# Norm statistics on ScalarE and attention sums over pairs of steps: a graph-attention kernel bound by TensorE

## The chip, the cores and the metric

One core of a Trainium2 chip. The metric is the device time of one execution in microseconds (us). Times are medians of several executions; all of this study's executions are of the fast state, with granted TensorE clocks of 0.985 to 0.996. A ratio is the mean time of one kernel's runs over that of the other's of the same rounds, so it is not quite the ratio of the two medians. Its interval is a 95% interval.

In lines of the profile PE is TensorE, PEld its weight loads, DVE VectorE, ACT ScalarE, POOL GpSimd and SPq the queue that issues transfers (DMA); L1108 is line 1108 of that run's kernel. A timeline line gives the start in us, the length in us, engine, line, operation, what it writes and reads, shapes and count; square brackets give the idle time of the engine before it and what ended it.

## The reference

Sixteen graphs of 1024 nodes with 256 channels pass four layers, each `x = x + layer(relu(layernorm(x)))`. Three are graph attention (4, 1 and 1 heads), the fourth is masked attention with 8 heads and a feed-forward part that ends in a norm of its own.

```python
h = relu(_layernorm(x)); x = x + _L0_gnn_ref(h, adj, W, a)       # 4 heads
h = relu(_layernorm(x)); x = x + _L1_gnn_ref(h, adj, W, a)       # 1 head
h = relu(_layernorm(x)); x = x + _L2_gnn_ref(h, adj, W, a)       # 1 head
h = relu(_layernorm(x))
# _L3_gnn_ref(h): 8 heads of 32 channels
scores = where(adj > 0, q @ k.T / sqrt(D), -1e9)
t = softmax(scores) @ v
y = _layernorm(h + t) * g1 + c1
x = x + _layernorm(y + relu(y @ w1 + b1) @ w2 + b2) * g2 + c2
```

## The kernel before

The kernel first records every operation of all batches, with an estimated duration and a priority, and then lists them greedily: each engine takes, of what is ready, the operation with the smallest priority. The lists are fixed when the program is built. On the chip each engine works through its own list in order. The priorities come from a few knots (values between which it interpolates) per stage, shifted by a lead per engine:

```python
LANDING = 2.5                       # assumed us from a DMA's end of transfer to its use
BIAS = 0.648                        # weight of TensorE's cost of changing its array shape
LEAD = {"act": -0.527, "dve": 0.112}

def priority(x):
    base, knots, total, lead = x.stream          # base is the batch number
    ...
    return round(key - (LEAD.get(x.engine, 0.0) if lead else 0.0), 6)
```

Statistics of every norm were taken on VectorE:

```python
def stats(src, src_ref, dst, dst_ref, whose="g"):
    st = r_st[whose].new()
    dve(0.342, lambda: nc.vector.bn_stats(st.t, src), [st], [src_ref])
    dve(0.11, lambda: nc.vector.bn_aggr(dst, st.t), [dst_ref], [st])
```

The attention of the fourth layer runs in four groups per batch (two sets of four heads, two halves of the queries), each of eight steps over the keys. In a step TensorE makes four score matmuls, ScalarE takes their exps, VectorE multiplies by the mask, and TensorE multiplies by the values ("va") in a "quad": four matmuls side by side, each in 32 columns of the array. The sum of the weights for the softmax comes from a quad with ones. In a "paired" group VectorE first adds two steps, so that one quad of ones serves both:

```python
def paired(g, hf):
    return g == 1 or hf == 1        # the first group is not paired
...
both = not paired(g, hf)
pe((1 + both) * 0.855, lambda: value(m, both), ...)      # quad of va, and of ones if not paired
if not both and jt % 2:
    pe(0.855, lambda: quad(accs[g, hf][1], jt, ..., lambda r: ones, ...), ...)
...
if paired(g, hf) and jt % 2:
    for ss, p0, p1 in zip(sums[n], pas[n - 1], pas[n]):
        dve(tt_us(2 * HALF), lambda: nc.vector.tensor_add(ss.t, p0.t, p1.t), [ss], [p0, p1])
```

The last stage reads the rows of x back, adds the last norm's constant row, and later stores from the same buffer (a ring of two, `r_xr`):

```python
dma(1.15, lambda: nc.sync.dma_start(xr.t, x3.t[:, it : it + 2, :]), [xr(0), xr(1)], [x3(hf)])
dve(tt_us(2 * C), lambda: nc.vector.tensor_add(xr.t, xr.t, rows["c2"].to_broadcast([P, 2, C])), ...)
...
dma(0.65, lambda: nc.sync.dma_start(out[b]...[:, it : it + 2, :], xr.t), [], [xr(0), xr(1)])
```

## Time and profile before

| | before |
|---|---|
| time, median of 3 | 4209.74 us (4208.88 to 4213.89) |
| TensorE, VectorE, ScalarE busy | 98%, 88%, 55% |
| one batch in the steady part | 255.5 us |
| end of the last batch's layer-3 products to the end of the span | 197 us |

Busy shares are averages over a start, a steady part in which two batches interleave, and an end in which the last batch is alone. The lines that carry the reading stand in the prediction.

### The profile page before, as it was taken

What the parts mean: (1) busy time and instruction counts of PE and PEld (TensorE: products, weight loads), DVE (VectorE), ACT (ScalarE), POOL (GpSimd) and SP (SyncE); (2) the same over time, 40 slices, a digit from 0 to 9 for tenths busy, and PEclk for the clock granted to TensorE, in tenths of its full rate; (3) what the DMA queues carried; (4) which work ended last, traced back from release to release, by engine and by line L of the source; (5) the groups of instructions that cost most, each with busy time, mean ns of one, the idle gap of its engine ahead of it and who ended that gap; (6) DMA issues with size and microseconds to landing.
All of it is one profiled execution on the core that took longest, in us unless ns stands there. A gap on an engine that the chain in (4) does not pass through costs nothing.

```text
span 4208.8 us, 68595 instructions
## 1 busy us (share of the span) xinstructions
PE 4133.7 (98%) x24738; PEld 2399.0 (57%) x24738; DVE 3710.0 (88%) x6786; ACT 2333.7 (55%) x5041; POOL 427.2 (10%) x391
## 2 busy tenths in 40 slices
PE   7999999999999999999999999999999999999998
PEld 3746556564665646556465564646656465564643
DVE  7589898998989889898998979989898898989977
ACT  3445555564655746556555555646556465565564
POOL 0001001011010101001010010110111010010110
PEclk9999999999999999999999999999999999999998
DMA  3121222212222122221212222122221222212131
GB/s 104 48 64 42 81 61 66 66 36 81 58 74 61 51 65 57 76 71 52 66 45 81 61 66 66 36 81 59 73 60 50 65 58 76 69 49 67 44 86 36
DMA packets 180683, 263.82 MB, mean 63 GB/s; under 512 B 41328, under 2 KB 76400, under 8 KB 180336
## 3 DMA queue, kind: packets, MB, share of 16 engines
q1 hardware_dynamic: 180336, 259.36, 22.5%
q8 instruction: 198, 3.24, 0.3%
q14 instruction: 149, 1.22, 0.1%
HBM read 91.03 MB, written 33.95 MB: 30 GB/s over the span
## 4 chain that ended last, share of the span: by engine, by line
PE 80%; DVE 12%; DMA 2%; SPq 2%; issue 2%; POOL 1%; ACT 1%; DVEq 0%; ACTq 0%
PE bank L801 21%; PE bank L1108 16%; PE sc L1235 10%; PE bank L677 8%; DVE pt L774 7%; PE bank L875 6%; PE bank L474 5%; PE sc L1024 5%; PE bank L1341 4%; PE bank L885 3%; DVE pa L1268 2%; PE sc L1060 2%; SPq L1045 2%; DMA row<-rd 1%; POOL rstdz L426 1%
## 5 line engine op out<-in xcount | busy, mean ns | idle before, releaser
L1259 ACT ACTIVATE pa<-sc 128x512 f32<-128x512 f32 x2048 | 1096.4, 607 | 588.4 <-PE sc L1235 448.6
L1268 DVE TENSOR_TENSOR pa<-pa,mask 128x1024 f32<-128x1024 f32 x1024 | 1210.1, 1211 | 12.4 <-ACT pa L1259 12.0
L774 DVE SCALAR_TENSOR_TENSOR pt<-row,e,mask 128x512 f32<-128x512 f32 x1536 | 1058.5, 740 | 107.5 <-DMA row<-rd 78.6
L801 PE MATMUL bank<-qb,pt 128*128 128x257 f32 x4096 | 942.8, 381 | 0.5 <-ACT ex L829 0.4
L801 PEld LDWEIGHTS bank<-qb,pt 128*128 128x128 f32 x4096 | 770.6, 190 | 166.5 <-issue 21.8
L1235 PE MATMUL sc<-qs,ks 128*128 128x512 f32 x2048 | 700.4, 448 | 1.9 <-ACT pa L1259 1.3
L1108 PE MATMUL bank<-pa,va 128*32 128x512 f32 x4096 | 543.5, 597 | 7.4 <-DVE pa L1268 7.0
L875 PE MATMUL bank<-pt,qb 128*32 128x512 f32 x4096 | 511.5, 596 | 4.7 <-DVE pt L774 4.7
L1235 PEld LDWEIGHTS sc<-qs,ks 128*128 128x128 f32 x2048 | 358.0, 188 | 223.7 <-ACT pa L1259 102.7
L1283 DVE TENSOR_TENSOR sums<-pa,pa 128x1024 f32<-128x1024 f32 x384 | 454.6, 1213 | 7.0 <-PE bank L1108 6.5
L677 PE MATMUL bank<-w_aug,hT 128*128 128x259 f32 (+1 forms) x1536 | 372.8, 391 | 0.6 <-ACT mask L587 0.2
L426 POOL TENSOR_TENSOR rstd<-rstd,neg_half 128x4 f32<-128x4 f32 x160 | 200.7, 1257 | 1499.8 <-DVE rstd L423 1340.9
L677 PEld LDWEIGHTS bank<-w_aug,hT 128*128 128x128 f32 x1536 | 289.4, 192 | 94.4 <-issue 15.3
L875 PEld LDWEIGHTS bank<-pt,qb 128*32 128x32 f32 x4096 | 132.8, 109 | 303.4 <-issue 210.3
L829 ACT ACTIVATE ex<-bank,rec 128x256 f32<-128x256 f32 x256 | 121.6, 476 | 324.0 <-DVE rec L821 321.1
L885 PE MATMUL bank<-pt,e 128*32 128x512 f32 x2048 | 288.4, 593 | 0.0
L1108 PEld LDWEIGHTS bank<-pa,va 128*32 128x32 f32 x4096 | 118.8, 109 | 283.1 <-issue 196.5
L445 ACT ACTIVATE hn<-xt,mv,rstd 128x256 f32<-128x256 f32 x384 | 204.2, 598 | 87.7 <-DVE mv L435 87.7
L906 ACT COPY ot<-bank 128x512 f32<-128x512 f32 x128 | 75.0, 586 | 318.7 <-PE bank L875 269.7
L1024 PE MATMUL sc<-hTa,wqkv_sb 128*128 128x512 f32 x512 | 239.9, 595 | 1.0 <-ACT hTa L1009 0.5
L1108 PE MATMUL bank<-sums,ones 128*32 128x512 f32 x1536 | 216.4, 597 | 0.7
L417 DVE BATCH_NORM_STATS2 stg<-xt 128x6 f32<-128x256 f32 x512 | 208.9, 414 | 3.2
(107 smaller groups left out, 4053.0 us busy)
## 6 DMA issues: line engine op xcount, KB each, us to landing
row<-rd SPq DMA_DIRECT2D x192, 256.0 KB
ks<-hi SPq DMA_DIRECT2D x512, 64.0 KB
ks<-lo SPq DMA_DIRECT2D x512, 64.0 KB
qs<-hi SPq DMA_DIRECT2D x512, 64.0 KB
qs<-lo SPq DMA_DIRECT2D x512, 64.0 KB
xt<-in_x_dram SPq DMA_DIRECT2D x32, 512.0 KB
x<-xt SPq DMA_DIRECT2D x32, 512.0 KB
xr<-x SPq DMA_DIRECT2D x64, 256.0 KB
```

Source lines behind the costliest of these rows:

```text
L426: lambda: nc.gpsimd.tensor_tensor(out=rstd, in0=rstd, in1=neg_half[:, :n], op=ALU.pow),
L677: nc.tensor.matmul(g.t[:, : C + 3 * H], hT.t[:, ct, k * P : (k + 1) * P], w_aug[l][:, ct, :], start=ct == 0, stop=ct == CT - 1,)
L774: lambda: nc.vector.scalar_tensor_tensor(pt.t, row.t, e3[:, 2, jt // TH, h, jt % TH : jt % TH + 1], mask[:, jt, hf * HALF : (hf + 1) * HAL ...
L801: nc.tensor.matmul(g.t[:, : D + 1], pts[jt].t[:, k * P : (k + 1) * P], qb[:, jt, 0, :], start=jt == 0, stop=jt == NT - 1,)
L875: nc.tensor.matmul(g.t[u * D + d : u * D + d + D3, :], qb[:, j, h + u, d : d + D3], pts[u][j - jt].t, start=j == 0, stop=j == NT - 1,)
L885: nc.tensor.matmul(gd.t[c : c + D3, :], one(jt + k, h + u).to_broadcast([P, D3]), pts[u][k].t, start=jt == 0, stop=jt == NT - 2,)
L1024: nc.tensor.matmul(sc.t, wqkv_sb[:, ct, c0 : c0 + P], hT.t[:, ct, hf * HALF : (hf + 1) * HALF], start=ct == 0, stop=ct == CT - 1,)
L1108: nc.tensor.matmul(ac.t[r * D3 : (r + 1) * D3, :], columns(r), of_head(r), start=first, stop=last,)
L1235: nc.tensor.matmul(scs[r - r0].t, ks.t[:, r, jt * P : (jt + 1) * P].bitcast(F32R), q.t[:, r, :].bitcast(F32R), start=True, stop=True,)
L1259: lambda: nc.scalar.activation(pt.t[:, v, :], sc.t, AF.Exp, scale=1.0 / math.sqrt(D3)),
L1268: lambda: nc.vector.tensor_mul(pt.t, pt.t, mask[:, jt : jt + 1, i0 : i0 + HALF].to_broadcast([P, 2, HALF]),),
L1283: lambda: nc.vector.tensor_add(ss.t, p0.t, p1.t),
```

## The change

The intent: take statistics off VectorE, which is 88% busy, give them to ScalarE, which is 55% busy, and spend what VectorE gains on pairing all sums, which takes quads of ones off TensorE. In the last batch, where VectorE is the fuller engine, nothing is paired. All priorities are set anew.

```diff
-BIAS = 0.648
-LEAD = {"act": -0.527, "dve": 0.112}
+BIAS = 0.977
+LEAD = {"act": 2.43, "dve": 0.791}
 ...  (all knots of GATS, VALUES, STEPS and FEED are new)
+    waste = ring("waste", 1, [C]).new()
+    SQUARED = (0, 2, 3,)
+    def spread_of(srcs, src_refs, sums, squares, refs):
+        act(0.19, lambda: nc.scalar.mul(sums, sums, -1.0 / C), refs, [])
+        for k, (src, src_ref, ref) in enumerate(zip(srcs, src_refs, refs)):
+            act(act_us(C, 1) + 60e-3,
+                lambda: nc.scalar.activation(waste.t, src, AF.Square,
+                    bias=sums[:, k : k + 1], accum_out=squares[:, k : k + 1]), [ref], [src_ref])
 ...  (one-head layers: the last residual operation gives the sum as well)
-                    stats(xs, xt(it), mv[:, l + 1, it, :], b_mv((l + 1, it)))
+                    dve(stt_us(C) + 60e-3,
+                        lambda: nc.vector.scalar_tensor_tensor(
+                            xs, xs, 0.0, last, op0=ALU.add, op1=op, accum_out=total), ...)
 ...
-            return g == 1 or hf == 1
+            return b < NB - 1
 ...  (last norm: two copies out of PSUM with a sum each, instead of one copy)
-                act(act_us(HALF), lambda: nc.scalar.copy(z_t, pz()), [z(0), z(1)], [g])
-                    stats(z_t[:, k, :], z(k), mvz.t[:, k, :], mvz(k), "f")
+                        lambda: nc.scalar.activation(
+                            z_t[:, k, :], pz()[:, k, :], AF.Copy, accum_out=mvz.t[:, k, 0:1])
 ...  (input norm)
-        for it in range(NT):
-            stats(xt.at(it), xt(it), b_mv.t[:, 0, it, :], b_mv((0, it)))
+            for it in its:
+                act(act_us(C) + 60e-3, lambda: nc.scalar.activation(
+                        waste.t, xt.at(it), AF.Copy, accum_out=b_mv.t[:, 0, it, 0:1]), ...)
+            spread_of(...)
```

The norms of the second layer's input and of the attention's sum keep bn_stats.

More of the change, by code (lines that the diff above doesn't have):

```diff
@@ L313, in direct @@
     GATS = (
-        (-0.447, -0.367, -0.162, 0.113, 0.24),
-        (0.384, 0.522, 0.626, 0.731, 0.828),
-        (0.805, 0.841, 0.856, 0.879, 1.02),
-    )
-    VALUES = (1.045, 1.057, 1.088, 1.245, 1.191)
-    STEPS = (1.289, 1.484, 1.664, 1.807, 1.951)
-    FEED = (2.178, 2.28, 2.353, 2.529, 2.38)
+        (-3.014, -2.567, -1.878, -0.484, 0.173),
+        (0.132, 0.454, 0.649, 0.709, 0.772),
+        (0.836, 0.897, 0.92, 0.922, 1.169),
+    )
+    VALUES = (1.226, 1.309, 1.09, 1.477, 0.846)
+    STEPS = (1.141, 1.486, 1.711, 1.952, 1.974)
+    FEED = (2.264, 2.344, 2.373, 2.44, 2.31)
     const = ctx.enter_context(tc.tile_pool(name="const", bufs=1))
@@ L418, in stats, with inverse_of_squares @@
         dve(0.11, lambda: nc.vector.bn_aggr(dst, st.t), [dst_ref], [st])
+    SQUARED = (0, 2, 3,)
+    def spread_of(srcs, src_refs, sums, squares, refs):
+        act(0.19, lambda: nc.scalar.mul(sums, sums, -1.0 / C), refs, [])
+        for k, (src, src_ref, ref) in enumerate(zip(srcs, src_refs, refs)):
+            act(
+                act_us(C, 1) + 60e-3,
+                lambda: nc.scalar.activation(
+                    waste.t, src, AF.Square, bias=sums[:, k : k + 1], accum_out=squares[:, k : k + 1]
+                ),
+                [ref],
+                [src_ref],
+            )
+    def inverse_of_squares(mean, squares, rstd, refs, rstd_ref, negate=True):
+        n = squares.shape[-1]
+        dve(
+            ts_us(n),
+            lambda: nc.vector.tensor_scalar(
+                rstd, squares, 1.0 / C, EPS, op0=ALU.mult, op1=ALU.add
+            ),
+            [rstd_ref],
+            refs,
+        )
+        pool(
+            0.98,
+            lambda: nc.gpsimd.tensor_tensor(
+                out=rstd, in0=rstd, in1=neg_half[:, :n], op=ALU.pow
+            ),
+            [rstd_ref],
+            [],
+        )
+        if negate:
+            dve(tt_us(n), lambda: nc.vector.tensor_mul(mean, mean, rstd), refs, [rstd_ref])
     def inverse(mean, var, rstd, mv_refs, rstd_ref, negate=True):
@@ L645, in gat @@
             mv_refs, rstd_ref = [b_mv((l, it)) for it in its], b_rstd((l, hf))
-            inverse(mv[:, l, s, 0], mv[:, l, s, 1], rstd[:, l, s], mv_refs, rstd_ref)
+            inv = inverse_of_squares if l in SQUARED else inverse
+            inv(mv[:, l, s, 0], mv[:, l, s, 1], rstd[:, l, s], mv_refs, rstd_ref)
             hn, hT = r_hn.new(), r_hT.new()
@@ L849, in gat @@
                     xs = xt.at(it)
-                    dve(tt_us(C), lambda: nc.vector.tensor_add(xs, xs, ex), [xt(it)], [b_ex(0)])
-                    if l != 1:
-                        dve(
-                            tt_us(C),
-                            lambda: nc.vector.tensor_sub(xs, xs, eo),
-                            [xt(it)],
-                            [b_ex(1)],
-                        )
-                    stats(xs, xt(it), mv[:, l + 1, it, :], b_mv((l + 1, it)))
+                    total = mv[:, l + 1, it, 0:1]
+                    if l == 1:
+                        last, op = ex, ALU.add
+                    else:
+                        dve(tt_us(C), lambda: nc.vector.tensor_add(xs, xs, ex), [xt(it)], [b_ex(0)])
+                        last, op = eo, ALU.subtract
+                    dve(
+                        stt_us(C) + 60e-3,
+                        lambda: nc.vector.scalar_tensor_tensor(
+                            xs, xs, 0.0, last, op0=ALU.add, op1=op, accum_out=total
+                        ),
+                        [xt(it), b_mv((l + 1, it))],
+                        [b_ex(int(l != 1))],
+                    )
+                its = range(hf * TH, (hf + 1) * TH)
+                spread_of(
+                    [xt.at(it) for it in its],
+                    [xt(it) for it in its],
+                    mv[:, l + 1, s, 0],
+                    mv[:, l + 1, s, 1],
+                    [b_mv((l + 1, it)) for it in its],
+                )
                 continue
@@ L982, in attention @@
             mv_refs, rstd_ref = [b_mv((3, it)) for it in its], b_rstd((3, hf))
-            inverse(mv[:, 3, s, 0], mv[:, 3, s, 1], rstd[:, 3, s], mv_refs, rstd_ref)
+            inv = inverse_of_squares if 3 in SQUARED else inverse
+            inv(mv[:, 3, s, 0], mv[:, 3, s, 1], rstd[:, 3, s], mv_refs, rstd_ref)
             for it in its:
@@ L1420, in back @@
                 pe(0.109 * 2 * CT, turn_back, [g], [yT])
-                act(act_us(HALF), lambda: nc.scalar.copy(z_t, pz()), [z(0), z(1)], [g])
                 for k in range(2):
-                    stats(z_t[:, k, :], z(k), mvz.t[:, k, :], mvz(k), "f")
-                inverse(
-                    mvz.t[:, :, 0], mvz.t[:, :, 1], rstdz.t, [mvz(0), mvz(1)], rstdz, False
+                    act(
+                        act_us(C) + 60e-3,
+                        lambda: nc.scalar.activation(
+                            z_t[:, k, :], pz()[:, k, :], AF.Copy, accum_out=mvz.t[:, k, 0:1]
+                        ),
+                        [z(k), mvz(k)],
+                        [g],
+                    )
+                refs = [mvz(0), mvz(1)]
+                spread_of(
+                    [z_t[:, k, :] for k in range(2)],
+                    [z(k) for k in range(2)],
+                    mvz.t[:, :, 0],
+                    mvz.t[:, :, 1],
+                    refs,
                 )
+                inverse_of_squares(mvz.t[:, :, 0], mvz.t[:, :, 1], rstdz.t, refs, rstdz, False)
                 for k in range(2):
@@ L1435, in back @@
                             rows["g2"][:, 0, :],
-                            op0=ALU.subtract,
+                            op0=ALU.add,
                             op1=ALU.mult,
@@ L1478, in batch @@
             )
-        for it in range(NT):
-            stats(xt.at(it), xt(it), b_mv.t[:, 0, it, :], b_mv((0, it)))
+        for hf in range(2):
+            its = range(hf * TH, (hf + 1) * TH)
+            for it in its:
+                act(
+                    act_us(C) + 60e-3,
+                    lambda: nc.scalar.activation(
+                        waste.t, xt.at(it), AF.Copy, accum_out=b_mv.t[:, 0, it, 0:1]
+                    ),
+                    [b_mv((0, it))],
+                    [xt(it)],
+                )
+            s = slice(hf * TH, (hf + 1) * TH)
+            spread_of(
+                [xt.at(it) for it in its],
+                [xt(it) for it in its],
+                b_mv.t[:, 0, s, 0],
+                b_mv.t[:, 0, s, 1],
+                [b_mv((0, it)) for it in its],
+            )
         for l in range(3):
```

## The prediction

> **What bounds the kernel now.** I read the page's engine shares first, then the groups by line and shape, then TensorE's own timeline, then the windows of the start and the end.
>
> ```profile
> span 4208.8 us, 68595 instructions
> PE 4133.7 (98%) x24738; PEld 2399.0 (57%) x24738; DVE 3710.0 (88%) x6786; ACT 2333.7 (55%) x5041; POOL 427.2 (10%) x391
> ```
>
> TensorE looks full, but the busy share of matmuls can mislead, so I measured it from distances between starts. In the timeline of TensorE (start, length, line, count):
>
> ```profile
> 1003.84 1.04 PE L885 MATMUL bank<-pt,e 128*32 128x512 f32 x8
> 1004.69 1.12 PE L1108 MATMUL bank<-pa,va 128*32 128x512 f32 x8
> 1005.55 1.12 PE L1108 MATMUL bank<-pa,ones 128*32 128x512 f32 x8
> 1006.60 1.09 PE L474 MATMUL bank<-ident,ot 128*128 128x128 f32 x8
> ```
>
> A "quad" (four matmuls side by side in 32-column strips, eight records because each fp32 matmul is two) takes 0.86 us from start to start, though the row says 1.12. I took the whole timeline from 400 to 3700 us and fitted, by least squares over the start-to-start distances, one duration for each kind of matmul and one for each kind of change between array shapes (full array, 32-column strips, the score matmuls). Result: 3189 us of matmuls, 70 us of changes of shape, 29 us of anything else, in 3289 us. So 97% of the steady part is matmul time and about 2.3 us per batch of some 255.6 us is waiting. (In the chain of work that ended last, the 12.18 us piece of L801 starts at 654.85 and, 13 batches later, at 3977.35: 255.6 us per batch.) The steady part is bound by TensorE's work. VectorE has 229 of 255 us filled in one batch, ScalarE 145.
>
> ```profile
> 455.00:710.00 255.00, 253.71 (x1544) 148.60 (x1543) 229.69 (x420) 144.89 (x314) 27.74 (x24) 1.00 0.23 63
> 4080.00:4120.00 40.00, 38.86 (x172) 13.74 (x168) 39.76 (x41) 24.07 (x46) 0.00 (x0) 1.00 0.39 97
> 4120.00:4160.00 40.00, 38.51 (x199) 13.14 (x198) 40.00 (x38) 24.84 (x48) 0.00 (x0) 1.00 0.06 14
> ```
>
> These windows give PE, PEld, DVE, ACT and POOL in turn. At the end, where the last batch is alone, the bound is another: from 4080 to 4160 VectorE has 79.8 of 80 us filled, and TensorE's pieces, counted with the fitted durations, are only about 54 us plus some 10 of changes.
>
> **What the Trainium skill says.**
> 1. "Perfetto Trace Analysis", opening note: matmul busy time is a bad measure, because matmuls are pipelined. Agreed here: 1.12 us recorded against 0.86 from start to start.
> 2. "TensorEngine Tiling (Array Packing)", Key Properties: changing the tiling mode drains TensorE. Agreed: in the fit a trip from the scores to the strips and back costs about 0.41 us, from the full array to the strips and back 0.22, and from the full array to the scores and back about nothing.
> 3. "ScalarE: Activation LUTs", What ACT_TABLE_LOAD costs: an ACTIVATE takes 186 ns plus 0.833 ns per element, plus 93 ns for each per-partition operand, and neighbours overlap by about 93 ns. For 256 elements that is 399 and 492 ns; the trace has 425 (no such operand, L843) and 476 (one, L829). It does not price the accumulator output. The built programs have one table load each, so Square brings no table switching.
> 4. "VectorE: DVE Perf Modes", Two Vector instructions with no wait between them: an op that writes out its accumulator is two instructions. No run shows it yet; I put 60 ns on it, as the kernel's own estimate does.
>
> **The change part by part.**
>
> ```profile
> L1268 DVE TENSOR_TENSOR pa<-pa,mask 128x1024 f32<-128x1024 f32 x1024 | 1210.1, 1211 | 12.4 <-ACT pa L1259 12.0
> L1283 DVE TENSOR_TENSOR sums<-pa,pa 128x1024 f32<-128x1024 f32 x384 | 454.6, 1213 | 7.0 <-PE bank L1108 6.5
> L1108 PE MATMUL bank<-sums,ones 128*32 128x512 f32 x1536 | 216.4, 597 | 0.7
> L1108 PE MATMUL bank<-pa,ones 128*32 128x512 f32 x1024 | 149.5, 593 | 0.0
> L417 DVE BATCH_NORM_STATS2 stg<-xt 128x6 f32<-128x256 f32 x512 | 208.9, 414 | 3.2
> L418 DVE BATCH_NORM_AGGREGATE mv<-stg 128x2 f32<-128x6 f32 x512 | 84.6, 168 | 2.3
> L850 DVE TENSOR_TENSOR xt<-xt,ex 128x256 f32<-128x256 f32 x256 | 105.8, 413 | 19.0 <-ACT ex L829 19.0
> ```
>
> (a) Attention sums. Each batch has four groups of eight steps. Before, the first group sums with one quad per step, the other three add pairs of steps on VectorE and take four quads. After, in 15 batches the first group is paired too: 4 quads less, 4 x 0.862 = 3.45 us per batch, 51.7 us in all, all on the bound engine. VectorE gets 8 adds more per batch, 8 x 1.213 = 9.7 us. The last batch loses its 24 adds (29 us of VectorE) and gets 12 quads (10.3 us).
>
> (b) Statistics. Gone from VectorE are 512 bn_stats (input, two layers, last norm) and as many aggregates: 384 x 0.414 + 128 x 0.408 + 512 x 0.167 = 297 us. The residual adds of two layers become scalar_tensor_tensor with an accumulator: 256 of them, about 0.468 (L1431, same size) + 0.06 against 0.413, so + 29 us. With the 96 more adds of (a), 116 us, VectorE's sum is -297 + 29 + 116 = -152, from 3710 to about 3560. In a steady batch: 229 + 9.7 - 18.5 + 1.8 = 222 us.
>
> (c) ScalarE gets 128 copies with a sum (about 0.485), 512 squares (0.536), 160 tiny scalings (0.19), and 64 copies of 512 are split in two: 62 + 274 + 30 + 22 = about 390 us of recorded time. From 145 to some 167 us of a batch. Off the path on average.
>
> (d) Order. All priorities are retuned. I compared the two built instruction streams: in batches 2 to 15 TensorE changes its array shape more often, 1353 times against 1177 over the 11 batches I counted alike. Weighted with the fitted costs, this is 71.7 against 59.9 us, 1.07 us per batch, 16 us over 15 batches. In the last batch's tail there are 72 changes against 84.
>
> (e) The tail. Where the last batch's first group runs unpaired, a step takes 3.0 us:
>
> ```profile
> 4055.13 1.33 PE L1235 MATMUL sc<-qs,ks 128*128 128x512 f32 x4
> 4056.39 1.06 PE L1108 MATMUL bank<-pa,va 128*32 128x512 f32 x8
> 4057.27 1.04 PE L1108 MATMUL bank<-pa,ones 128*32 128x512 f32 x8
> 4058.24 1.20 PE L1235 MATMUL sc<-qs,ks 128*128 128x512 f32 x4
> ```
>
> The other 24 steps now take from 4074 to 4166, 91.5 us, with VectorE full. Unpaired they take 24.5 x 3.0 = 73.5, plus about 10 for projections and transposes between: 83. I count -8 us.
>
> Sum: -51.7 + 16 - 8 = -44 us, so 4166 from 4210. For the start I add and take nothing: TensorE waits there for chains of single steps (about 50 of the first 190 us), some of which get longer by the squares and some shorter on VectorE.
>
> **The rivals.**
> 1. *The squares get in front of the exps.* Ten blocks per batch of up to four squares and a scaling, about 2 us each, stand in ScalarE's queue, and only four banks hold scores; TensorE's order is fixed, so a late exp stops it. For it: the largest wait of TensorE's weight loads on another engine is for L1259 (102.7 us). Against: ScalarE still has a third of its time free, and the squares stand early in their streams with slack. If each block cost 0.3 us, 10 x 0.3 x 16 = 48 us: no gain, about 4210.
> 2. *VectorE becomes the bound in the first group.* 9.7 us more fall into one quarter of the attention. For it: 88% busy. Against: it has less to do in the whole batch (222 of 252), and other groups already run so. If half of the added time showed, 4.9 x 15 = 73 us: about 4240.
> 3. *Less VectorE load removes waits too.* All that is not matmul or change of shape in the steady part is 29 us; if it halved, and the tail gave 15 instead of 8, about 4145.
>
> **Range and chances.** The removed quads are certain, the added changes are counted from the streams, though their cost is a fit. Unsure are the waits, from -20 to +30. Hence 4166, range 4138 to 4194. A gain over 2% needs below 4125.5, some 40 us more than I can name: 0.06. Slower than 4294 would need both first rivals in full: 0.01. Within 2%: 0.93.
>
> **What would show it.** Right: the steady distance between batches falls to about 253.2 us; ones matmuls fall to 256 + 1920 records; sums on VectorE are 480; the last batch shows 3.0 us steps to its end and VectorE no longer full there; ScalarE's busy time is near 2700 us, VectorE's near 3560. Wrong: many idle stretches of TensorE that end with L1259's exps or with the pair adds (rivals 1 and 2), squares over 0.7 us each, or a fit of the new timeline in which changes of shape cost much more or less than 16 us over before.

## The result, and the profile after

| | before | after |
|---|---|---|
| time, median of 4 each | 4211.11 us | 4185.22 us (4183.66 to 4186.84) |
| ratio after / before | | 0.9938 (0.9921 to 0.9955) |

The change is 26 us or 0.6% faster, clear of noise and within 2%. The prediction was 4166 with a range of 4138 to 4194: the sign and the range hold, and the gain is a little more than half of the 44 us forecast.

The page of the changed kernel, its span and engine shares:

```profile
span 4181.8 us, 68682 instructions
PE 4111.5 (98%) x24354; PEld 2359.1 (56%) x24354; DVE 3627.9 (87%) x6114; ACT 2682.7 (64%) x6673; POOL 469.3 (11%) x391
```

Its groups by line and shape, the answers to the lines of before. After the bar come the busy time in us, the mean of one in ns, then the idle time of the engine before them.

```profile
L1336 DVE TENSOR_TENSOR sums<-pa,pa 128x1024 f32<-128x1024 f32 x480 | 573.2, 1221 | 4.4 <-PE bank L1161 1.0
L1161 PE MATMUL bank<-sums,ones 128*32 128x512 f32 x1920 | 262.3, 597 | 0.0
L1161 PE MATMUL bank<-pa,ones 128*32 128x512 f32 x256 | 36.4, 607 | 0.0
L429 ACT ACTIVATE waste<-xt,mv 128x256 f32<-128x256 f32 x384 | 196.3, 511 | 9.3
L429 ACT ACTIVATION_READ_ACCUMULATOR waste<-xt,mv 128x1 f32 x384 | 73.2, 191 | 0.0
L897 DVE SCALAR_TENSOR_TENSOR xt<-xt,ex 128x256 f32<-128x256 f32 x256 | 107.7, 421 | 24.2 <-ACT ex L868 20.0 <-ACT ex L882 3.7
L897 DVE DVE_READ_ACCUMULATOR xt<-xt,ex 128x1 f32 x256 | 21.6, 84 | 0.0
```

The reader sees the counts that the change promises: 480 pair adds, 1920 records of ones over sums, 256 over single steps. Each operation with an accumulator has a second, short instruction behind it. The windows of the steady part and of the end (PE, PEld, DVE, ACT, POOL):

```profile
455.00:710.00 255.00, 254.47 (x1517) 147.46 (x1516) 228.19 (x383) 167.81 (x420) 30.25 (x24) 1.00 0.23 64
4080.00:4120.00 40.00, 39.01 (x239) 14.94 (x238) 30.53 (x29) 26.02 (x51) 0.00 (x0) 1.00 0.30 73
4120.00:4160.00 40.00, 39.84 (x235) 17.01 (x235) 27.58 (x52) 28.85 (x64) 2.78 (x4) 1.00 0.00 1
```

At the end VectorE falls from 40 to about 29 of 40 us.

**One account for all kernels.** To compare kernels I use the prediction's fit. Each matmul record gets the duration that the kernel before shows from start to start (score matmul 0.230 us, record of a quad 0.108, transpose 0.117, 512-column record 0.418, 257-column record 0.218), and each change of array shape its fitted cost. What is left of TensorE's timeline is "rest": waits, plus what the fit misses. The account counts the records and changes that a profile shows; it does not measure their cost anew. It is good to some 0.2 us: kernels with the same records per batch differ in its matmuls by 0.15 us (the kernel before, and the statistics with new priorities below) and 0.19 us (the changed kernel, and pairing alone). The limits of the batches are the ends of the layer-3 products (L801 before, L840 after). Per batch, over the 13 batches from the second's limit to the fifteenth's:

| us per batch | period | matmuls | changes of shape | rest |
|---|---|---|---|---|
| before | 255.52 | 247.55 | 5.45 | 2.52 |
| after | 253.70 | 244.10 | 6.52 | 3.08 |

And over the profiled spans, from these limits:

| us | start to batch 0's limit | batch 0's to batch 15's limit | from there to the end | span |
|---|---|---|---|---|
| before | 190.3 | 3821.2 | 197.3 | 4208.8 |
| after | 192.7 | 3796.4 | 192.7 | 4181.8 |
| difference | +2.4 | -24.8 | -4.6 | -27.0 |

### The profile page after: what moved, and what is told of

Same layout as the page of the kernel before. It is cut to its first block, busy times and chain, and to the rows that moved or that the text cites. A ratio compares the mean times of both kernels' runs of the same rounds, so it can differ in the third digit from the quotient of the medians.

```text
span 4181.8 us, 68682 instructions
## 1 busy us (share of the span) xinstructions
PE 4111.5 (98%) x24354; PEld 2359.1 (56%) x24354; DVE 3627.9 (87%) x6114; ACT 2682.7 (64%) x6673; POOL 469.3 (11%) x391
## 4 chain that ended last, share of the span: by engine, by line
PE 80%; DVE 14%; POOL 2%; ACT 2%; issue 2%; DMA 1%; SPq 0%; DVEq 0%; ACTq 0%; POOLq 0%
PE bank L840 19%; PE bank L1161 15%; PE sc L1288 10%; PE bank L927 10%; PE bank L716 6%; PE bank L512 5%; PE sc L1077 5%; PE bank L937 5%; DVE pa L1321 4%; PE bank L1394 3%; DVE sums L1336 3%; PE sc L1113 3%; DVE pt L813 3%; POOL rstd L464 1%; POOL rstdz L449 1%
## 5 line engine op out<-in xcount | busy, mean ns | idle before, releaser
L840 PE MATMUL bank<-qb,pt 128*128 128x257 f32 x4096 | 939.9, 381 | 0.0
L840 PEld LDWEIGHTS bank<-qb,pt 128*128 128x128 f32 x4096 | 770.7, 189 | 155.7 <-issue 26.0
L1288 PE MATMUL sc<-qs,ks 128*128 128x512 f32 x2048 | 746.5, 462 | 5.1 <-ACT pa L1312 1.8
L1336 DVE TENSOR_TENSOR sums<-pa,pa 128x1024 f32<-128x1024 f32 x480 | 573.2, 1221 | 4.4 <-PE bank L1161 1.0
L1161 PE MATMUL bank<-pa,va 128*32 128x512 f32 x4096 | 513.2, 598 | 6.5 <-DVE pa L1321 6.5
L716 PE MATMUL bank<-w_aug,hT 128*128 128x259 f32 (+1 forms) x1536 | 406.8, 396 | 3.0 <-ACT hT L710 2.4
L868 ACT ACTIVATE ex<-bank,rec 128x256 f32<-128x256 f32 x256 | 121.7, 475 | 434.8 <-DVE rec L860 433.0
L449 POOL TENSOR_TENSOR rstd<-rstd,neg_half 128x4 f32<-128x4 f32 x96 | 129.6, 1350 | 1546.3 <-DVE rstd L441 1445.9
L937 PE MATMUL bank<-pt,e 128*32 128x512 f32 x2048 | 278.4, 592 | 0.0
L1161 PE MATMUL bank<-sums,ones 128*32 128x512 f32 x1920 | 262.3, 597 | 0.0
L1161 PEld LDWEIGHTS bank<-pa,va 128*32 128x32 f32 x4096 | 109.6, 109 | 250.0 <-issue 197.5
L429 ACT ACTIVATE waste<-xt,mv 128x256 f32<-128x256 f32 x384 | 196.3, 511 | 9.3
```

The lines of the kernel that those rows point to most:

```text
L716: nc.tensor.matmul(g.t[:, : C + 3 * H], hT.t[:, ct, k * P : (k + 1) * P], w_aug[l][:, ct, :], start=ct == 0, stop=ct == CT - 1,)
L840: nc.tensor.matmul(g.t[:, : D + 1], pts[jt].t[:, k * P : (k + 1) * P], qb[:, jt, 0, :], start=jt == 0, stop=jt == NT - 1,)
L937: nc.tensor.matmul(gd.t[c : c + D3, :], one(jt + k, h + u).to_broadcast([P, D3]), pts[u][k].t, start=jt == 0, stop=jt == NT - 2,)
L1161: nc.tensor.matmul(ac.t[r * D3 : (r + 1) * D3, :], columns(r), of_head(r), start=first, stop=last,)
L1288: nc.tensor.matmul(scs[r - r0].t, ks.t[:, r, jt * P : (jt + 1) * P].bitcast(F32R), q.t[:, r, :].bitcast(F32R), start=True, stop=True,)
```

## The experiments

Twelve kernels ran. They fall into four questions: which part of the change does what, how much room ScalarE has, what the tail holds, and what keeps it from holding more. All are correct but one. One combination couldn't be built: with the new priorities and neither part, the greedy listing finds no complete order.

### Which part does what

**Pairing alone, old priorities.** The kernel before with

```diff
-            return g == 1 or hf == 1
+            return b < NB - 1
```

> Only the pairing of part (a), with the priorities and the VectorE statistics of before. Theory 1 (TensorE's matmul time is the bound and VectorE has room): 41 us of quads go and the last batch gains some 8 us, so about 4165. Rival (VectorE becomes the bound in the first group, since it gets 116 us more and nothing is taken from it, 3826 us of busy time, 91%): waits of the exps' and quads' buffers eat half or more, 4190 to 4215.

Measured: 4297.18 us, ratio 1.0205 (1.0191 to 1.0219). Slower than even the rival said. The quads did go (matmuls 243.91 us per batch), but changes of shape rose to 8.37 and rest to 10.72 us. In the list of waits from 700 to 3500 us, ScalarE's exps (L1259) stand longer behind buffers that VectorE's pair adds (L1283) have not yet released. First the kernel before, then this run, in the same window (engine, line, what it waited for; us in total, times, longest):

```profile
ACT pa L1259 <- DVE sums L1283: 30.6, 16, 2.5
```

```profile
ACT pa L1259 <- DVE sums L1283: 88.9, 43, 4.2
```

In the same list of this run exps wait 109.8 us for the last norm's statistics (mvz, L418), a pair that the kernel before does not show in that window. So exps wait for VectorE, which works through its list in order and is 89% busy.

**Statistics alone, old priorities.** The changed kernel with the old pairing and the old numbers:

```diff
-            return b < NB - 1
+            return g == 1 or hf == 1
 (and BIAS, LEAD and all knots as before)
```

> Only the statistics moved to ScalarE, with the pairing and the priorities of before. Theory 1 (ScalarE is off the path and TensorE's work is unchanged): 4200 to 4212, with VectorE's busy time down by about 270 us. Rival (squares in front of the exps stop TensorE): 4225 to 4260, with the fitted time of one score matmul up from 0.230 us to 0.240 or more.

Measured: 4291.68 us, ratio 1.0195 (1.0181 to 1.0209). Theory 1 falls here: TensorE's matmuls are unchanged, VectorE's busy time is 175 us less, and the kernel is 80 us slower. Rest is 6.62 and changes 6.39 us per batch. The number that the rival named, the time at the score matmuls, did not grow as it said: by the account, what is left behind them in the steady part is 9.8 us in all, against 16.4 before. The largest piece of rest, 29 us, is at the transposes of the attention's norm.

**Both, old priorities.** The whole change with the old numbers only.

> Both parts, with the priorities of before. If the new priorities are what makes the parts pay, it is at 4200 or above. If they only trim, it is at 4180 to 4195, beside 4185 for the whole change. If the extra changes of array shape (16 us) come from the new priorities alone, it could be as fast as 4170.

Measured: 4233.42 us, ratio 1.0053 (1.0039 to 1.0067): slower than before. Pairs cost 86 us alone, statistics 80 alone, together they would cost 166 if they added up, and they cost 22. They mend each other. Changes of shape are 7.93 us per batch, more than the 6.52 of the whole change. So the extra changes that I had counted in the new list come with the parts under the old priorities already, and the new priorities lower them.

**Statistics and new priorities, old pairing.** The whole change with

```diff
-            return b < NB - 1
+            return g == 1 or hf == 1
```

> The whole change without its pairing (the first group of every batch unpaired, the others paired, the last batch too). If the gain of the whole change lies in the quads that went, this is slower than it by 41 us plus some 5 for the tail, 4225 to 4232, slower than the kernel before. If the gain lies in less work on VectorE or in the new priorities, it is at 4190 to 4205.

Measured: 4243.87 us, ratio 1.0076 (1.0063 to 1.009). The whole change is 59 us below this, more than the 41 us of quads. Per batch 3.30 us is matmuls by the account (the four quads are 3.45); changes take 0.32 back, and rest gives 0.26. The remaining 16 us is the tail: 208.6 us here, 192.7 with the last batch unpaired.

**Pairing and new priorities, old statistics.** The kernel before with the new pairing and the new numbers.

> Pairing and the new priorities, with the statistics left on VectorE. If the room that the statistics leave on VectorE is what lets the pairing pay, this is far above the whole change: with old priorities the pairs alone were at 4297; trimming priorities took 48 us off twice, so about 4250, at the least 4230. If the new priorities were all that was needed, 4185 to 4200.

Measured: 4309.55 us, ratio 1.0234 (1.022 to 1.0248). The new numbers do not help here at all; they cost 12 us more than the old ones. From here, moving the statistics is worth 124 us. My guess that the new numbers would take some 48 us off any version is wrong.

The five runs and the two kernels side by side:

| us | old priorities | new priorities |
|---|---|---|
| neither part | 4210 to 4212 (before) | no order found |
| pairing | 4297 | 4310 |
| statistics on ScalarE | 4292 | 4244 |
| both | 4233 | 4185 (after) |

Only one cell of this table beats the kernel before. With these two sets of numbers neither part gains alone, and both together gain only with the new ones. That is not yet proof that pairing needs the moved statistics: the old numbers were set for neither part and the new ones for both, so each part alone ran with numbers set for another kernel. No run gives one part priorities of its own, and how much of its 80 us is the part and how much the numbers stays open.

### How much room ScalarE has

**Each square twice, same lists.** Each square is issued twice in a row; the listing still takes its old duration, so the order on TensorE, GpSimd and, but for two rows, VectorE is that of the whole change.

```diff
-                lambda: nc.scalar.activation(waste.t, src, AF.Square, ...),
+                lambda: [nc.scalar.activation(waste.t, src, AF.Square, ...) for _ in range(2)],
```

> The whole change with each square issued twice in a row (same result, same order on every engine, 512 more squares on ScalarE, about 250 us of its time). Theory (in the changed kernel the score matmuls wait a little for exps that stand behind squares: 237 ns each in the fit against 230 before): slower by 25 us or more, 4210 or above, and the score matmuls' fitted time grows by 10 ns or more. Rival (ScalarE's third of free time takes it): at most 5 us slower, 4190 or below.

Measured: 4435.07 us, ratio 1.0533 (1.0518 to 1.0547). 512 squares with their accumulator reads are about 0.49 us each from start to start (4013.91 to 4014.40 in ScalarE's timeline of the whole change), 251 us, and the kernel is 250 us slower. The page says:

```profile
PE 4225.9 (95%) x24354; PEld 2376.0 (54%) x24354; DVE 3637.5 (82%) x6114; ACT 2983.0 (67%) x7697; POOL 434.4 (10%) x391
```

ScalarE is 67% busy, and still nothing of the added time was absorbed. The granted clock is a little lower here (0.985 to 0.987, against 0.994 to 0.995), but that isn't the reason: half of all transposes still follow each other within 0.109 us, as in the whole change. A third of idle time on an engine is no room if its list is fixed and others wait on it.

**A quarter of each square, same lists.** Wrong: the variance is taken from 64 of 256 channels.

```diff
-                    waste.t, src, AF.Square, ...
+                    waste.t[:, : C // 4], src[:, : C // 4], AF.Square, ...
-                rstd, squares, 1.0 / C, EPS, ...
+                rstd, squares, 4.0 / C, EPS, ...
```

> The whole change with each square taken over 64 of the 256 elements and the sum scaled by four, same order everywhere; the result is wrong on purpose (a sampled variance). ScalarE loses 512 times 0.16 us, 82 us. If waits for ScalarE hold the gain back, 5 to 10 us faster than the whole change, 4175 to 4180. If not, 4182 to 4186.

Measured: 4180.81 us (4176.93 to 4182.14), ratio 0.9926 (0.9913 to 0.994), with a relative error of 0.048 as intended. ScalarE's busy time fell by 74 us, and the steady part did not move: period 253.63 against 253.70, rest 3.16 against 3.08. The ratio's interval overlaps that of the whole change. So at its present load ScalarE's square time is not what holds the steady part back. My theory that score matmuls wait for exps behind squares falls in so far as the length of the squares is meant; the waits for exps themselves are still there (see "The waits" below), and this run left the copies with a sum, the scalings and the accumulator reads at their length. Together with the run before: of 251 us more, 250 show, and of 74 us less, nothing shows in the steady part. So the whole change seems to sit close to the load from which more time for squares costs in full.

**Each square twice, and the listing knows.** As the first of these, with the duration doubled in the listing:

```diff
-                act_us(C, 1) + 60e-3,
+                2 * (act_us(C, 1) + 60e-3),
```

> Each square issued twice as in the run that was 250 us slower, but the order is worked out with the doubled duration, so the queues are laid around it. If ScalarE truly has no room left (its 64% busy time being all it can give), this is as slow as the unplanned one, 4420 to 4440. If only the fixed order had no room for time it did not know of, ScalarE's busy share rises to about 70% and most of the 250 us goes: 4200 to 4290.

Measured: 4356.96 us, ratio 1.0349 (1.0335 to 1.0363). It lies between my two readings, and neither is right. Knowing of the time saves 78 of the 250 us; 172 us stay, with ScalarE at 68%. Changes of shape are 9.32 and rest is 11.86 us per batch. Whether priorities set for this load would save more, no run shows.

### The tail

**Last batch paired too.**

```diff
-            return b < NB - 1
+            return True
```

> The whole change with the last batch paired like the others. The prediction gave the unpaired last batch 8 us; the two runs with the old priorities that leave it unpaired have tails 15 to 17 us shorter than those that pair three of its groups. So 4193 by the first, 4200 by the second; if VectorE isn't the bound there, 4175 to 4185, since 16 quads less are to be done.

Measured: 4207.57 us, ratio 0.9993 (0.9979 to 1.0007). The steady part is the same (253.74 us), and the tail is 213.9 us instead of 192.7. So leaving the last batch unpaired is worth 22 us against pairing all of it, and 16 us against pairing three of its groups (the run with statistics and new priorities). The old priorities show the same: tails of 184.6 with both parts and unpaired, 202.1 with statistics and three groups paired.

That also shows a cost: with the new priorities the unpaired tail is 8 us longer than with the old (192.7 against 184.6). In the tail of the whole change TensorE stands for 6 us at the start of the last batch's attention. First TensorE's timeline, then VectorE's:

```profile
4029.68 1.05 PE L1161 MATMUL bank<-pa,va 128*32 128x512 f32 x4
4036.68 1.07 PE L1161 MATMUL bank<-pa,va 128*32 128x512 f32 x2 [5.96 <-DVE pa L1321]
```

```profile
4029.45 0.69 DVE L1452 TENSOR_TENSOR xr<-xr,row_c 128x512 f32<-128x512 f32 x1 [4.25 <-DMA xr<-x]
4030.06 0.48 DVE L1496 SCALAR_TENSOR_TENSOR fz<-fz,mvz,row_g 128x256 f32<-128x256 f32 x1
4033.67 0.69 DVE L1452 TENSOR_TENSOR xr<-xr,row_c 128x512 f32<-128x512 f32 x1 [3.13 <-DMA xr<-x]
4034.28 2.36 DVE L1321 TENSOR_TENSOR pa<-pa,mask 128x1024 f32<-128x1024 f32 x2
```

The mask multiplications that TensorE needs stand in VectorE's list behind two additions (L1452) to re-read rows. Their loads wait for stores from the same buffers, which land after 4.1 and 3.6 us in the chain of work.

**Three buffers for the rows.** To make room, the squares' unused output is kept as bytes and the column of ones is shared.

```diff
-    waste = ring("waste", 1, [C]).new()
-    r_xr = ring("xr", 2, [2, C])
+    waste = Buf(work.tile([P, C], U8, name="waste"), [])
+    r_xr = ring("xr", 3, [2, C])
-    ones = work.tile([P, D3], F32, name="ones")
+    ones = ones_col.to_broadcast([P, D3])
```

> The whole change with three buffers instead of two for the rows that the last stage reads back (room from the squares' unused output kept as bytes and from a shared column of ones). In the changed kernel's tail VectorE stands behind such a load, which waits for the store from the same buffer, and TensorE waits 6 us for masks. If that chain is the cause of the hole, it goes: 4176 to 4180. If the hole has another cause or the order takes another, 4183 to 4188.

Measured: 4177.32 us (4174.41 to 4181.22), ratio 0.9921 (0.9908 to 0.9935). The time is as expected, but not by the expected cause: TensorE's timeline still has the hole (5.74 us at 4029.84), because the load still waits 4.2 us for a store, and the tail is 192.9 us. The 8 us are 0.4 us per batch in the steady part (253.31) and about 1 us at the start. Which of the three edits brings them is not separated, and the listing gave another order as well (1612 changes of shape in the 13 batches, against 1599). This is the fastest kernel, though its interval overlaps that of the whole change.

**The row's addition on GpSimd.** The whole change with L1452 moved:

```diff
-                dve(tt_us(2 * C), lambda: nc.vector.tensor_add(xr.t, xr.t, rows["c2"]...), ...)
+                pool(1.1, lambda: nc.gpsimd.tensor_tensor(out=xr.t, in0=xr.t, in1=rows["c2"]..., op=ALU.add), ...)
```

> The whole change with the addition of the norm's last row to the re-read rows moved from VectorE to GpSimd. With a third buffer the 6 us hole of TensorE at the start of the last batch stayed: VectorE still stood behind that addition, which waits for a load of 3.3 us that itself waits 4.1 us for a store. If VectorE's place in the queue is the cause of the hole, it goes here: 4174 to 4180, and 64 times 0.69 us of VectorE with it. If GpSimd is late with the sum, the stage's own end moves and nothing is won, 4183 to 4195.

Measured: 4213.99 us, ratio 1.0009 (0.9995 to 1.0022). The hole is gone. At the place where it was, TensorE goes straight on:

```profile
4065.62 1.03 PE L1288 MATMUL sc<-qs,ks 128*128 128x512 f32 x2
4066.58 1.13 PE L1161 MATMUL bank<-pa,va 128*32 128x512 f32 x6
```

A stretch of 2.3 us is left at 4072.5, which ends with VectorE's L1089 and the transfer that this waits for. The tail is 187.3 us, 5.4 shorter. So the additions' place in VectorE's list is the cause of the hole. But the steady period is 256.26 us, 2.6 longer, with rest at 5.82. The addition takes 1.62 us there (0.68 on VectorE), and GpSimd's list now stands behind loads:

```profile
L1452 POOL TENSOR_TENSOR xr<-xr,row_c 128x512 f32<-128x512 f32 x64 | 103.9, 1624 | 266.5 <-DMA xr<-x 193.9 <-DVE rstdz L441 48.9 <-DVE reca L1248 12.5
```

GpSimd also makes the inverse roots of all norms, in order behind these. That this is what lengthens the steady part is likely, but not shown by a run of its own.

**Both, but GpSimd in the last batch but one only.**

```diff
+                add_row(
+                    *((pool, 1.5, nc.gpsimd) if b == NB - 2 else (dve, tt_us(2 * C), nc.vector))
+                )
```

> Three row buffers, and the row's addition on GpSimd in the last batch but one only; elsewhere VectorE does it as in the whole change. Moving it everywhere closed the 6 us hole (none of TensorE's idle stretches there had it, and the tail was 5 us shorter) but cost 2.5 us in each other batch. If the hole comes from VectorE's place in the queue alone, the gain stays without that cost: 5 to 7 us faster than the run with three buffers (4177), 4170 to 4172, and the fastest of all. If the hole only moves, 4176 to 4179.

Measured: 4178.57 us, ratio 0.9923 (0.991 to 0.9937): no gain over three buffers alone. The steady part stayed at 253.30 us, but the hole did too:

```profile
4032.95 0.69 DVE L1452 TENSOR_TENSOR xr<-xr,row_c 128x512 f32<-128x512 f32 x1 [7.80 <-DMA xr<-x]
```

One addition was still on VectorE there. Only the batch before the last had been moved, so this one belongs to the last batch, whose rows are fetched ahead. With one left, the hole is as long as before (6.02 us). I moved one addition too few; a version that moves both was not run.

## Why the prediction was right or wrong, point by point

**What binds the kernel: right.** The steady part follows TensorE's work. The profile shows 32 quad records less per batch, as forecast. That the account gives 3.45 us for them (247.55 to 244.10) is no second measurement, since it uses the forecast's own durations. What is measured is the period, 1.82 us shorter.

**The changes of array shape: counted right, wrong in origin.** 1.07 us per batch were forecast from the built lists, and the account gives 1.07 (5.45 to 6.52): the same lists at the same fitted costs, so this shows only that the chip ran what was listed. And I called them the cost of the retuned priorities. With the old priorities both parts make 7.93. The parts bring them under the old priorities too, and the new priorities lower them.

**The waits: mis-sized.** The prediction left them as they were. They rose by 0.56 us per batch (2.52 to 3.08), 7 us over 13 batches. Where they rose can be read from the trace. In the 13 batches of the kernel before, the third and the fourth score matmul of a group start within 0.26 us of the one in front, with one exception. In the changed kernel three of them start late in every batch, by up to 0.49 us and always in the same two groups; against the usual 0.23 us these late starts add up to 0.55 us per batch. This fits the sums: 1.82 us of period and these 0.55 are 2.37, and quads less changes were 3.45 - 1.07 = 2.38. The weight load in front waits for an exp, and that exp stands in ScalarE's list behind other work. One of the two places, first the weight load, then ScalarE's list:

```profile
1700.87 0.19 PEld L1288 LDWEIGHTS sc<-qs,ks 128*128 128x128 f32 x1 [0.30 <-ACT pa L1312]
```

```profile
1697.61 0.49 ACT L868 ACTIVATE ex<-bank,rec 128x256 f32<-128x256 f32 x1
1697.96 0.51 ACT L876 ACTIVATE ex<-bank,rec 128x256 f32<-128x256 f32 x1
1698.32 0.45 ACT L1549 ACTIVATE waste<-xt 128x256 f32<-128x256 f32 x1
1698.63 0.24 ACT L1549 ACTIVATION_READ_ACCUMULATOR waste<-xt 128x1 f32 x1
1698.72 2.10 ACT L1312 ACTIVATE pa<-sc 128x512 f32<-128x512 f32 x4
```

So rival 1 had the right wait, but not its cause: no square stands in front here, and with squares of a quarter the late starts are 0.55 us as before. L1549 is a copy with a sum that the change has put on ScalarE, L868 and L876 were there before. With both parts and the old priorities these late starts are 0.03 us per batch. So they come with the new order; which of the operations in front makes the difference, no run shows. Rival 3, that less work on VectorE removes waits, did not come about, and its basis was too large: I took 152 us off VectorE, and its busy time fell by 82. By groups, its rows sum to 127 us less; the rest had lain in overlaps, as the records of short operations partly cover their neighbours.

**The tail: too small a term, and one that was missing.** I gave the unpaired last batch 8 us, by counting 3.0 us steps over the stretch in which VectorE was full (24.5 of them, where there are 24). It is worth 16 us against the old pairing. The tails of the runs give the other terms: 197.3 us before, 202.1 with the statistics moved, 208.6 with the new priorities too, 192.7 with the last batch unpaired. So the moved statistics took 5 us back and the new priorities 6.5 (8 with the last batch unpaired, 6 of them at the hole in front of VectorE's row additions). That the sum, 4.6 us, comes near my 8 is luck.

**The start: 0 forecast, +2.4 us measured.**

**The steps side by side**, in us of the profiled spans: quads and changes in batches 1 to 15, forecast -51.7 + 16 = -36, and -24.8 measured for the whole of these batches, waits included; tail -8, measured -4.6; start 0, measured +2.4. Sum -44 against -27. Of the 17 us that are missing, 11 lie in batches 1 to 15 (7 of them are the waits of the 13 steady batches, 4 lie in the first and the last of the 15 and are not taken apart), 3 in the tail and 2 at the start. The largest step that failed is the zero for waits.

**Rival 2, VectorE as the bound: wrong for the whole change, supported for pairing alone.** With pairing and no moved statistics the kernel lost 2%, and exps waited longer for VectorE, though with priorities not set for it. The prediction judged the parts as if each had its own price. They do not: the loss of either alone is near 80 us and of both together 22, before the priorities are set.

**ScalarE "has a third of its time free": wrong as an argument.** It was true of the busy share, and it did little harm only because the load stayed close to what its list bears.

## What to carry to other kernels

Where lists are fixed, judge an engine's room by adding work to it, not by its idle share: here 251 us more on an engine that was 64% busy cost 250 us, and 74 us less won nothing in the steady part. Try parts of a change together and with priorities set anew before dropping one: two parts that cost 2% each under the old priorities gave 0.6% together under new ones. Count the bound engine's work from the built lists with durations taken from start to start: here that gave 2.38 us per batch, and 1.82 came, because waits grew by 0.55. Waits don't follow from such a count, and each place where an in-order engine stands behind a transfer has to be looked for by itself.

## What the Trainium skill lacked or had wrong

- "Trainium Kernel Development and Optimization", Best Practices, says that for engines other than TensorE occupancy is fine as a measure of the distance to the roofline. For ScalarE here it is not a measure of room: at 64% busy, 251 us more of work cost 250 us (and 172 us when the order was built for it).
- "ScalarE: Activation LUTs", What it computes, names the accumulator output without a price. The trace has a second instruction of 191 to 229 ns behind each. A copy of 256 elements out of PSUM with its read (L1477) follows the one before at 0.35 to 0.37 us, a square with a per-partition operand at 0.49 us. The page's duration for such a square without the read, 492 ns, agrees with the 511 ns recorded.
- "VectorE: DVE Perf Modes", Two Vector instructions with no wait between them: the split of an operation with an accumulator into two instructions is confirmed, and no page gives the read's duration. It is 84 ns. The scalar_tensor_tensor of 256 elements in front of it took 421 ns, as long as the tensor_tensor of before (413), so the 468 ns that I took from another row was too long.
- "TensorEngine Tiling (Array Packing)", Key Properties: that changing the mode drains the array is in line with the fit, and no cost is given. Fitted here: about 0.41 us from score matmuls to 32-column quads and back, 0.22 us from the full array to the quads and back, nothing visible from the full array to the score matmuls and back.
